# Six homes for the transforms' channel groups, and the resizing products of both spectra later in the text

## The chip, the cores and the metric

The kernel runs on one core of a Trainium2 chip. TensorE (PE) multiplies matrices into PSUM, VectorE (DVE), ScalarE (ACT) and GpSimd (POOL) work on the elements, and SyncE (SP) only issues transfers; DMA transfers are also issued from the queues of ACT and POOL. PE loads its weights by instructions of their own (PEld). All engines run side by side, each through its own instructions in their order, and wait for each other on semaphores.

The metric is the device time of one execution in microseconds (us). Three executions of the kernel before took 9171.22, 9193.05 and 9202.3 us; the median, 9193.05, is the time before. The profile is of a further execution.

## The reference

The input is x, 32 images of 96 channels, 56x56, in float32. Two layers follow each other.

The first layer is a residual block: a 1x1 convolution to 576 channels, batch norm and silu; a depthwise 3x3 convolution, batch norm and silu; a squeeze (mean over the image, two small matrices, sigmoid) that scales the 576 channels; a 1x1 convolution back to 96 channels, batch norm, and x added. The weights go through a fake quantisation to 8 bits first.

The second layer takes the magnitude of an image's spectrum twice. Cut to what matters:

```
mag = abs(rfft2(x));  fe = mag.mean over channels
ca  = sigmoid(W2 relu(W1 pooled(conv(mag))))            # one factor a channel
s   = [x.mean(channels), sqrt((x*x).mean(channels) + 1e-6), resize(fe, 56x56)]
sa  = sigmoid(small convolutions of s)                  # one factor a pixel
y   = x * ca * sa
freq = resize(abs(rfft2(y)).mean over channels, 56x56)
aux = [y, 4 coordinate planes, freq]
offset, gate = 3x3 convolutions of aux;  y_base = 3x3 convolution of y
y_def = deformable 3x3 convolution: y sampled bilinearly at 9 offset taps
z   = (1 - gate) * y_base + gate * y_def
out = relu(batchnorm(z over the whole batch) + x)
```

Since the batch norm takes its statistics over all 32 images, the output is written in a last pass.

## The kernel before

The program has two streams of preparation and one main loop. The main loop goes through bands: an image is cut into 7 bands of 8 rows, 32 images make 224 bands, and each band is joined from offset and gate convolutions (L606), the base convolution (L635), hat tables that turn bilinear sampling into products (L671 to L699), transposes (L714), samples (L728, evacuated to `v` by ACT in L732 and L739) and deformable products (L747).

Beside the bands run two generators, `first(b + 2)` and `second(b + 1)`. `first` is the residual block's expansion and depthwise convolution (`hidden`, L169 to L262), whose result `h2d` goes to DRAM. `second` is `attend`: it loads the rows of `h2d` (`project_loads`, tiles `hq0` and `hq1`, L306), projects them (L324, L330), adds the residual, stores the block's result in DRAM (`x1`, L467/468), and then runs the attention of the second layer. The main loop calls `pump()` at each of the 119 slots of an image; `pump()` steps both generators in proportion to the time: a stream has a number of steps, a slot at which it begins and a slot at which it is due. `second` is due at `slot + length - 8`.

`attend` uses the transform `dft_mag` twice, once on x1 and once on y (with `gate=sa`). A transform has these steps:

- It loads 6 groups of 2 x 8 channels, [112 x 8 x 56], into padded tiles of [112 x 8 x 64] (L362). Three such tiles, `x2_0` to `x2_2`, are filled with zeros once by GpSimd at the start of the program and taken in rotation, so that group g + 3 can only be loaded when group g has been read. Groups 0 to 2 are requested at the transform's start, group g + 3 behind the products of group g.
- For y, GpSimd multiplies each group by sa (`weigh`, L367).
- PE multiplies each group by the first Fourier matrix (L387, four program products a group; the trace shows each fp32 product as two records), into a PSUM bank; ACT copies the result to `s1` (L394). For x1, ACT also squares the group into a PSUM bank (L371) and DVE sums the group and its squares over the channels (L373).
- PE applies the second Fourier matrix in three groups (L411), ACT squares (L414) into a tile of the pool `sq`, DVE adds (L415).
- ACT takes the square root (L418).

`resized_spectrum` follows: DVE (for y) multiplies by the channel factors `cx` (L427) and sums over the channels (L428, `m_fe` or `m_fy`), PE applies the resizing matrix (L431) and ACT copies the result (L433, `fe` or `fy`). `fe` is read much later, in the small convolutions of `s` (L532 onward); in between DVE works out the channel attention (`edge` to `qs`, L486 to L498) and PE multiplies it through (L502, L508, L513), all in columns of one PSUM tile `pc`. `fy` is read by the next product (L573, `pz`), whose copy `fq` (L575) is stored by GpSimd's queue (L578) and loaded as one of the rows of aux (L597) for L606 of the next image.

PSUM has 8 banks: 6 in the rotating pool `mm` (taken by L169, L324, L371, L387, L411, L606, L635, L714, L728, L770), one in `acc` (the small products, L431 among them), one in `pd` (L747). SBUF pools of one buffer: `hq`, `sp`, `sq`, `s1p`; so the next user of such a tile waits for the last reader of the one before.

The order of the instructions on PE, DVE, ACT and POOL is set by a scheduler with a cost model of its own, which may move an instruction past others; SP's instructions stand in the order of the text. A `yield` in a generator sets how the two streams and the bands interleave in that text.

Of the kernel before, what the change touches and what calls it, by code (L numbers as in the profile page):

```python
# [7 lines left out]
FP = mybir.dt.float32  # L8
# [8 lines left out]
C, H, W = 96, 56, 56  # L17
HW = H * W
HID, RED = 576, 24
NCH = 5  # L20
# [13 lines left out]
EW = ER * W  # L34
# [25 lines left out]
CG = 8  # L60
# [240 lines left out]

def project_loads(nc, p, h2d, q, half):

    u0, u1 = ((0, NCH - 1), (NCH - 1, len(UNITS)))[half]
    hq = p["hq"].tile([128, u1 - u0, EW], FP, name=f"hq{half}")
    nc.sync.dma_start(hq, h2d[u0:u1, :, q * EW : (q + 1) * EW].rearrange("u p n -> p u n"))  # L306
    return [(UNITS[u][0], hq[:, u - u0]) for u in range(u0, u1)]
# [31 lines left out]
def dft_mag(nc, p, src, gate=None):  # L339
# [14 lines left out]
    x2s = []  # L354

    def load(g):
        if g < NG:
            x2 = p["x2"][p["n_x2"] % len(p["x2"])]
            p["n_x2"] += 1
            for half in range(2):  # L360
                c0 = half * C // 2 + g * CG
                nc.sync.dma_start(x2[half * H : (half + 1) * H, :, :W], hwc[:, c0 : c0 + CG])  # L362
            x2s.append(x2)
# [58 lines left out]
def resized_spectrum(nc, p, mag, name, scale=None):  # L422


    m2 = p["sp"].tile([2 * WX, V], FP, name=f"m_{name}")
    if scale is not None:
        nc.vector.tensor_tensor(mag, mag, scale.unsqueeze(2).to_broadcast([2 * WX, NP, V]), ALU.mult)  # L427
    nc.vector.tensor_reduce(m2, mag.rearrange("p q u -> p u q"), AX.X, ALU.add)  # L428
    yield
    pf = p["acc"].tile([128, 512], FP, name="acc")  # L430
    nc.tensor.matmul(pf[:V, : 2 * W], m2, p["w"]["RT2"], start=True, stop=True)  # L431
    rs = p["sp"].tile([V, 2, W], FP, name=name)
    nc.scalar.copy(rs.rearrange("p m w -> p (m w)"), pf[:V, : 2 * W])  # L433
    p["resized"] = rs
    yield


def attend(tc, p, b, x, h2d, pooled, x1, given=False):
# [43 lines left out]
    yield from resized_spectrum(nc, p, mag, "fe")  # L482
    fe = p["resized"]
# [28 lines left out]

    nc.tensor.matmul(pc[:C, 1:2], w["cp2"], c1[:MID], start=True, stop=True)  # L513
# [55 lines left out]
    yield from resized_spectrum(nc, p, p["magnitude"], "fy", cx)  # L569
    fy = p["resized"]  # L570
# [352 lines left out]
def padded(nc, p, a, images):  # L923

    cp = p["cp"]
    yps = [cp.tile([CJ, HY, WY], FP, name=f"yp{i}") for i in range(images)]
    for t in yps:
        nc.gpsimd.memset(t, 0.0)
        nc.sync.dma_start(t[C : C + 4, PD : PD + H, PD : PD + W], a["coord"])
        nc.sync.dma_start(t[CA:, PD : PD + H, PD : PD + W], a["place"])  # L930
    p["x2"], p["n_x2"] = [cp.tile([2 * H, CG, WX], FP, name=f"x2_{i}") for i in range(3)], 0
    for t in p["x2"]:
        nc.gpsimd.memset(t, 0.0)
    p["s4"] = [cp.tile([H, 3, WP], FP, name=f"s4_{i}") for i in range(2)]
    for t in p["s4"]:
        nc.gpsimd.memset(t, 0.0)
    return yps
# [8 lines left out]
def layers(tc, a, dp, x1d, zd, stats, far):  # L946
# [8 lines left out]
    with ExitStack() as ctx:  # L955
# [8 lines left out]
                                 ("ca", 2), ("s1p", 1), ("xc", 2), ("sp", 1), ("sq", 1), ("q1", 3), ("q2", 2), ("hid", 2), ("yb", 4),  # L964
# [11 lines left out]
        def second(b):  # L976
            if b >= B:
                return iter(())
            h2d, pooled = held.pop(b)
            return attend(tc, p, b, a["x"][b], h2d, pooled, x1d[b])  # L980
# [34 lines left out]
        def start(b, length):  # L1015
            streams[:] = [[second(b + 1), 0, n_second, slot + 3, slot + length - 8],
                          [first(b + 2), 0, n_first, slot, slot + length]]
# [238 lines left out]
def gather_block(tc, a, dp, x1d, zd, stats):  # L1256
# [4 lines left out]
    with ExitStack() as ctx:  # L1261
# [11 lines left out]
        pools(tc, ctx, p, None, (("ca", 1), ("s1p", 1), ("xc", 2), ("sp", 1), ("sq", 2), ("q1", 2), ("q2", 2),  # L1273
# [235 lines left out]
```

## Time and profile before

| | |
|---|---|
| median of 3 runs | 9193.05 us (9171.22 to 9202.3) |
| profiled execution: device time, span | 9212.26 us, 9210.5 us |
| mean granted clock of TensorE | 0.931 |
| PE busy, instructions | 8288.6 us (90%), 52406 |
| DVE busy | 7178.9 us (78%) |
| ACT busy | 5374.1 us (58%) |
| POOL busy | 2600.3 us (28%) |
| L362, loads of the groups | 768 issues of 98 KB each |
| L387, product of a group | 3072 records, 262 to 562 ns, median 275 |
| L431, resizing product, fe and fy | 64 records each, median 258 and 391 ns |
| L428, sum over the channels | 64 of 2520 to 2585 ns |
| L418, square root, and the table load ahead of it | 1.41 and 1.28 us in the second transform of one image |

The page gives the busy time of each engine, then the span in 40 slices with a digit of the busy share for each. A busy PE is not PE at its peak: matmul records overlap, their ends are modelled, and the clock that the chip grants to TensorE varies; the clock's slices (PEclk) stand in tenths of full speed. A row of the waits reads "engine, line, what it waited for: us in all, times, longest". A wait on an engine that isn't late for anybody costs nothing. A row of the timeline reads "start, duration, engine, line, operation, output <- inputs, count, [idle before <- what ended it]".

### The profile page before, as it was taken

The numbers are of one execution on the slowest core, as the hardware profiler recorded it, in microseconds if no ns is written. First come the engines' busy times: TensorE is split into PE (matmuls) and PEld (weight loads), VectorE is DVE, ScalarE is ACT, GpSimd is POOL, SyncE is SP. The second block draws the span as 40 slices with busy tenths as digits, with TensorE's granted clock in tenths as the row PEclk, the third lists the DMA queues.
The fourth block names the chain that finished last, engine by engine and source line by source line (L and its number), as shares of the span: only waits on it lengthen the run. The fifth ranks groups of instructions, "written<-read, shape, count | busy, mean of one in ns | idle before, by whom it ended". The sixth has DMA issues, their size and how long they took to land. (4 is left out here: it accounts for less than half of the span.)

```text
span 9210.5 us, 138071 instructions
## 1 busy us (share of the span) xinstructions
PE 8288.6 (90%) x52406; PEld 5229.5 (57%) x52406; DVE 7178.9 (78%) x6693; ACT 5374.1 (58%) x10486; POOL 2600.3 (28%) x2611
## 2 busy tenths in 40 slices
PE   5889999999999999999999999999999999999870
PEld 3455556565555656555565655555565556655550
DVE  7587888888788888888888888788888888887333
ACT  2355656666556666665566666566666656666553
POOL 0123233232323323232332333233223323332210
PEclk9889999999999999999999999999999999999985
DMA  2345655555556555555555555555555565555459
GB/s 85 94 136 158 165 167 161 160 154 152 157 164 167 162 158 152 153 158 164 166 162 162 151 152 161 163 165 157 161 147 157 159 166 166 161 164 140 127 181 418
DMA packets 1068764, 1486.54 MB, mean 161 GB/s; under 512 B 590190, under 2 KB 839838, under 8 KB 1055806
## 3 DMA queue, kind: packets, MB, share of 16 engines
q1 hardware_dynamic: 858995, 985.20, 40.1%
q10 hardware_dynamic: 153803, 329.80, 9.8%
q0 software_dynamic: 55296, 162.60, 6.8%
q8 instruction: 421, 6.90, 0.4%
q14 instruction: 249, 2.04, 0.1%
HBM read 1064.29 MB, written 412.65 MB: 160 GB/s over the span
## 5 line engine op out<-in xcount | busy, mean ns | idle before, releaser
L262 DVE SCALAR_TENSOR_TENSOR acch<-hp,w,acch 128x1512 f32<-128x1512 f32 (+1 forms) x2250 | 4397.4, 1954 | 35.7
L606 PE MATMUL mm<-yp,c_jointW 104*128 104x448 f32 x4032 | 1721.4, 580 | 4.8 <-DMA yp<-fqd 2.8
L710 POOL COPY ybl<-yp 96x448 f32<-96x448 f32 x896 | 1133.9, 1292 | 1736.1 <-PE mm L714 1735.9
L747 PE MATMUL pd<-v,c_def 128*96 128x224 f32 (+1 forms) x6272 | 1397.0, 370 | 17.8 <-ACT v L732 16.9
L606 PEld LDWEIGHTS mm<-yp,c_jointW 104*128 104x128 f32 x4032 | 796.9, 201 | 809.7 <-issue 775.0
L747 PEld LDWEIGHTS pd<-v,c_def 128*96 128x96 f32 (+1 forms) x6272 | 1028.3, 170 | 296.5 <-issue 78.5
L728 PE MATMUL mm<-wc,yt 64*96 64x144 f32 x12544 | 1093.4, 301 | 101.2 <-ACT hp L173 45.3
L173 ACT ACTIVATE hp<-mm,sh,inv 128x392 f32<-128x392 f32 (+2 forms) x1216 | 812.8, 673 | 567.3 <-PE mm L169 489.2
L169 PE MATMUL mm<-xt,w 96*128 96x392 f32 (+3 forms) x2688 | 1071.6, 537 | 37.8 <-DMA xt<-in_x 33.3
L728 PEld LDWEIGHTS mm<-wc,yt 64*96 64x96 f32 x12544 | 848.0, 164 | 416.8 <-issue 190.0
L732 ACT COPY v<-mm 96x288 f32<-96x288 f32 (+1 forms) x2688 | 1004.3, 443 | 98.9 <-PE mm L728 60.1
L699 DVE TENSOR_TENSOR wc<-wc,wr 128x1008 f32<-128x1008 f32 x448 | 575.2, 1284 | 570.1 <-DMA wr<-hd 515.7
L324 PE MATMUL mm<-hq,w3s 128*96 128x392 f32 x2048 | 800.8, 538 | 148.2 <-DMA hq<-h2d 145.8
L635 PE MATMUL mm<-yp,c_base0W 96*64 96x224 f32 x8064 | 827.7, 357 | 0.0
L739 ACT COPY v<-v 32x448 f32<-32x448 f32 x1344 | 755.2, 562 | 29.9
L635 PEld LDWEIGHTS mm<-yp,c_base0W 96*64 96x64 f32 x8064 | 553.6, 135 | 276.1 <-issue 71.6
L659 POOL DMA_DIRECT2D od<-at x224 | 185.9, 830 | 1788.0 <-DVE at L655 1247.6
L716 ACT COPY yt<-mm 128x384 f32<-128x384 f32 (+1 forms) x896 | 350.2, 440 | 520.4 <-PE mm L714 519.6
L324 PEld LDWEIGHTS mm<-hq,w3s 128*96 128x96 f32 x2048 | 341.2, 175 | 505.3 <-issue 472.7
L222 ACT ACTIVATE acch<-acch,sh,inv 128x1568 f32<-128x1568 f32 x288 | 488.5, 1696 | 192.4 <-DVE acch L262 182.3
L626 ACT ACTIVATE hid<-mm,c_dg1b 50x448 f32<-50x448 f32 x224 | 140.6, 627 | 744.3 <-PE mm L606 703.2
L467 POOL TENSOR_TENSOR o<-o,xc 96x392 f32<-96x392 f32 x256 | 369.6, 1444 | 677.3 <-ACT o L334 675.9
(194 smaller groups left out, 9065.7 us busy)
## 6 DMA issues: line engine op xcount, KB each, us to landing
h2d<-acch ACTq DMA_DIRECT2D x288, 784.0 KB
wc<-hd SPq DMA_DIRECT2D x896, 252.0 KB
wr<-hd SPq DMA_DIRECT2D x896, 252.0 KB
hq<-h2d SPq DMA_DIRECT2D x128, 980.0 KB
hq<-h2d SPq DMA_DIRECT2D x128, 784.0 KB
x<-x1d SPq DMA_DIRECT2D x768, 98.0 KB
ht<-od SPq DMA_DIRECT2D x224, 252.0 KB
hd<-ht ACTq DMA_DIRECT2D x224, 252.0 KB
```

The costliest lines, as they stand in the source:

```text
L169: nc.tensor.matmul(pt[p0 : p0 + w1.shape[1], : rows * W], w1, xts[hf][:, r0 * W : (r0 + rows) * W], start=True, stop=True)
L173: nc.scalar.activation(h1[lo:hi, row0 : row0 + rows, 1 : 1 + W], pt[lo:hi, : rows * W].rearrange("p (h w) -> p h w", h=rows), AF.Silu, bia ...
L262: nc.vector.scalar_tensor_tensor(acc[:, lo:hi], win, wk, acc[:, lo:hi], ALU.mult, ALU.add)
L324: nc.tensor.matmul(pts[half][:C, :EW], w3s[:, ch], hq, start=(i == 0), stop=False)
L606: nc.tensor.matmul(view, weights[:, k], yp[:channels, r0 : r0 + RB, dx + PD - 1 : dx + PD - 1 + W], start=(k == 0), stop=(k == NTAP - 1))
L635: nc.tensor.matmul(pb[i * BC : (i + 1) * BC, : BW // 2].rearrange("p (h w) -> p h w", h=RB // 2), w["base"][:, k], yp[:C, r0 + i * RB // 2 ...
L699: p["tc"].keep_in_program_order(nc.vector.tensor_tensor(wc, wc, wr, ALU.mult))
L710: nc.gpsimd.tensor_copy(yb[:, :, s], blocks)
L728: nc.tensor.matmul(pt[k][:C, (t - lo) * KP : (t - lo + 1) * KP], yt[ps, t], s[ps, t * KP : (t + 1) * KP], start=True, stop=True)
L732: nc.scalar.copy(v[:C, :, lo:hi, k].rearrange("c k t p -> c t k p"), pt[k][:C, : (hi - lo) * KP].rearrange("c (t k p) -> c t k p", t=hi - ...
L739: nc.scalar.copy(v[C:, 1 + 2 * i : 3 + 2 * i], v[i * QC : (i + 1) * QC, KA:])
L747: nc.tensor.matmul(out.rearrange("c q (t x) -> c t q x", x=TS), p["w"]["def"][ks, k], v[ks, k].rearrange("c t s (r x) -> c t (s r) x", r=T ...
```

## The change

The three tiles `x2_0` to `x2_2` go. Instead the six groups of a transform live in the two tiles of the projection's rows: groups 0 to 2 in `hq0`, groups 3 to 5 in `hq1`, each taken anew at the transform's start (a function `project_rows` gives the tile for both uses). As these tiles hold other data in between, the padding columns 56 to 63 of all six groups are zeroed by DVE at each transform's start: two memsets of [112 x 24 x 8] a transform.

The pool `sq` gets two buffers in place of one.

`resized_spectrum` is split. `summed_spectrum` keeps the scaling and the sum over the channels at their old place; the resizing product and its copy come later in the text. For fe they now stand after L508 (new numbers: the product is L440), directly ahead of the product of the channel attention's last matrix (L513, new L523), and the product writes columns 128 and up of the PSUM tile `pc`, not a tile of its own. For fy they stand one step later than before. `second` has one step more and is due at `slot + length - 6`.

A block at the end of the program that doesn't run for these inputs gets a pool `hq`, as `dft_mag` asks for it.

```diff
--- before.py
+++ after.py
@@ -299,10 +299,15 @@
     yield
 
 
+def project_rows(p, half):
+
+    return p["hq"].tile([128, (NCH - 1, len(UNITS) - NCH + 1)[half], EW], FP, name=f"hq{half}")
+
+
 def project_loads(nc, p, h2d, q, half):
 
     u0, u1 = ((0, NCH - 1), (NCH - 1, len(UNITS)))[half]
-    hq = p["hq"].tile([128, u1 - u0, EW], FP, name=f"hq{half}")
+    hq = project_rows(p, half)
     nc.sync.dma_start(hq, h2d[u0:u1, :, q * EW : (q + 1) * EW].rearrange("u p n -> p u n"))
     return [(UNITS[u][0], hq[:, u - u0]) for u in range(u0, u1)]
 
@@ -352,15 +357,16 @@
     if gate is None:
         parts = p["sq"].tile([2 * WX, 2, NPB * V], FP, name="sq")[: 2 * H, :, : NG * W].rearrange("p k (g w) -> p k g w", g=NG)
     x2s = []
+    for i in range(2):
+        rows = project_rows(p, i).rearrange("p u n -> p (u n)")[: 2 * H, : NG // 2 * CG * WX].rearrange("h (c w) -> h c w", w=WX)
+        nc.vector.memset(rows[:, :, W:], 0.0)
+        x2s.extend(rows[:, g * CG : (g + 1) * CG] for g in range(NG // 2))
 
     def load(g):
         if g < NG:
-            x2 = p["x2"][p["n_x2"] % len(p["x2"])]
-            p["n_x2"] += 1
             for half in range(2):
                 c0 = half * C // 2 + g * CG
-                nc.sync.dma_start(x2[half * H : (half + 1) * H, :, :W], hwc[:, c0 : c0 + CG])
-            x2s.append(x2)
+                nc.sync.dma_start(x2s[g][half * H : (half + 1) * H, :, :W], hwc[:, c0 : c0 + CG])
 
     def weigh(g):
         if gate is not None and g < NG:
@@ -419,20 +425,22 @@
     p["magnitude"] = mag
 
 
-def resized_spectrum(nc, p, mag, name, scale=None):
+def summed_spectrum(nc, p, mag, name, scale=None):
 
 
     m2 = p["sp"].tile([2 * WX, V], FP, name=f"m_{name}")
     if scale is not None:
         nc.vector.tensor_tensor(mag, mag, scale.unsqueeze(2).to_broadcast([2 * WX, NP, V]), ALU.mult)
     nc.vector.tensor_reduce(m2, mag.rearrange("p q u -> p u q"), AX.X, ALU.add)
-    yield
-    pf = p["acc"].tile([128, 512], FP, name="acc")
+    return m2
+
+
+def resized_spectrum(nc, p, m2, name, pf):
+
     nc.tensor.matmul(pf[:V, : 2 * W], m2, p["w"]["RT2"], start=True, stop=True)
     rs = p["sp"].tile([V, 2, W], FP, name=name)
     nc.scalar.copy(rs.rearrange("p m w -> p (m w)"), pf[:V, : 2 * W])
-    p["resized"] = rs
-    yield
+    return rs
 
 
 def attend(tc, p, b, x, h2d, pooled, x1, given=False):
@@ -479,8 +487,9 @@
     nc.scalar.activation(s3[:, 1], pm[:H, W : 2 * W], AF.Sqrt, bias=w["eps6"][:H], scale=1.0 / C)
     nc.scalar.mul(s3[:, 0], pm[:H, :W], 1.0 / C)
     yield
-    yield from resized_spectrum(nc, p, mag, "fe")
-    fe = p["resized"]
+    m_fe = summed_spectrum(nc, p, mag, "fe")
+    yield
+    yield
     mas = p["sp"].tile([2 * WX, 2, NP], FP, name="mas")
     edge = p["sp"].tile([2 * WX, NP, NE], FP, name="edge")
     nc.vector.tensor_copy(edge[:, :, :4], mag[:, :, :4])
@@ -510,6 +519,7 @@
     nc.scalar.activation(c1, pc[: 2 * MID, 0:1], AF.Relu, bias=w["cp1b"])
     yield
 
+    fe = resized_spectrum(nc, p, m_fe, "fe", pc[:, 128:])
     nc.tensor.matmul(pc[:C, 1:2], w["cp2"], c1[:MID], start=True, stop=True)
     c2 = p["sp"].tile([2 * MID, 2 * WX], FP, name="c2")
     nc.vector.tensor_scalar(c2, w["twoT"], c1, None, ALU.mult)
@@ -566,8 +576,11 @@
 
     yield from dft_mag(nc, p, x1, sa)
     yield
-    yield from resized_spectrum(nc, p, p["magnitude"], "fy", cx)
-    fy = p["resized"]
+    m_fy = summed_spectrum(nc, p, p["magnitude"], "fy", cx)
+    yield
+    yield
+    fy = resized_spectrum(nc, p, m_fy, "fy", p["acc"].tile([128, 512], FP, name="acc"))
+    yield
     pz = p["acc"].tile([128, 512], FP, name="acc")
     for m in range(2):
         nc.tensor.matmul(pz[:H, H : H + W], w["rows2"][:, m], fy[:, m], start=(m == 0), stop=(m == 1))
@@ -928,9 +941,6 @@
         nc.gpsimd.memset(t, 0.0)
         nc.sync.dma_start(t[C : C + 4, PD : PD + H, PD : PD + W], a["coord"])
         nc.sync.dma_start(t[CA:, PD : PD + H, PD : PD + W], a["place"])
-    p["x2"], p["n_x2"] = [cp.tile([2 * H, CG, WX], FP, name=f"x2_{i}") for i in range(3)], 0
-    for t in p["x2"]:
-        nc.gpsimd.memset(t, 0.0)
     p["s4"] = [cp.tile([H, 3, WP], FP, name=f"s4_{i}") for i in range(2)]
     for t in p["s4"]:
         nc.gpsimd.memset(t, 0.0)
@@ -961,7 +971,7 @@
         top = p["cp"].tile([NOFF, NBD + 1], FP, name="top")
         nc.gpsimd.memset(top, 0.0)
         pools(tc, ctx, p, None, (("xt", 2), ("acch", 2), ("pl", 2), ("w3s", 1), ("hq", 1), ("o", 2), 
-                                 ("ca", 2), ("s1p", 1), ("xc", 2), ("sp", 1), ("sq", 1), ("q1", 3), ("q2", 2), ("hid", 2), ("yb", 4),
+                                 ("ca", 2), ("s1p", 1), ("xc", 2), ("sp", 1), ("sq", 2), ("q1", 3), ("q2", 2), ("hid", 2), ("yb", 4),
                                  ("off", 1), ("st", 2), ("ht", 1), ("wc", READY + AHEAD + 1), ("wr", AHEAD + 1), ("yt", 2), ("ybl", 1),
                                  ("vp", 2)))
 
@@ -1013,7 +1023,7 @@
         turn = NBD - 2
 
         def start(b, length):
-            streams[:] = [[second(b + 1), 0, n_second, slot + 3, slot + length - 8],
+            streams[:] = [[second(b + 1), 0, n_second, slot + 3, slot + length - 6],
                           [first(b + 2), 0, n_first, slot, slot + length]]
 
         def pump():
@@ -1270,7 +1280,7 @@
             tz = table.rearrange("(p n) f -> p (n f)", p=116)
             for i in range(4):
                 nc.sync.dma_start(tz[:, i * zt.shape[1] : (i + 1) * zt.shape[1]], zt)
-        pools(tc, ctx, p, None, (("ca", 1), ("s1p", 1), ("xc", 2), ("sp", 1), ("sq", 2), ("q1", 2), ("q2", 2),
+        pools(tc, ctx, p, None, (("ca", 1), ("s1p", 1), ("xc", 2), ("sp", 1), ("sq", 2), ("hq", 1), ("q1", 2), ("q2", 2),
                                  ("hid", 2), ("off", 1), ("ix", 2), ("vp", 1), ("gp", 4), ("smp", 2)))
         with tc.For_i(0, B, 1) as b:
             st = p["sp"].tile([C, NBD, 6], FP, name="st")
```

## The prediction

> **What bounds the kernel now.** I read the page's busy shares and slices first, then the waits of TensorE (PE), of VectorE (DVE), of ScalarE (ACT) and of SyncE's queue (SP), then the timeline of one image.
>
> ```profile
> PE 8288.6 (90%) x52406; PEld 5229.5 (57%) x52406; DVE 7178.9 (78%) x6693; ACT 5374.1 (58%) x10486; POOL 2600.3 (28%) x2611
> PE   5889999999999999999999999999999999999870
> PEclk9889999999999999999999999999999999999985
> ```
> PE is busy 9 tenths or more in nearly every slice, at a clock that reads 9, not 10. So time comes back only from PE's idle stretches, from the slow stretches behind them, or from DVE where PE follows it. Which idle stretches does the change touch?
>
> ```profile
> PE mm L324 <- DMA hq<-h2d: 145.8, 30, 7.0
> PE acc L431 <- DVE m_fe L428: 64.0, 31, 2.7
> PE mm L387 <- DVE sq L373: 54.9, 19, 4.2
> PE acc L431 <- DVE m_fy L428: 51.7, 32, 11.3
> PE mm L387 <- DMA x<-x1d: 42.7, 13, 11.0
> PE mm L387 <- POOL x L367: 18.1, 29, 3.4
> ACT sq L414 <- DVE s L415: 216.7, 50, 7.2
> SPq L362 <- PE mm L387: 924.8, 124, 50.7
> ```
> Columns: microseconds in all, times, longest. The largest, L324 for its rows, is not touched. L431, the resizing product, is both times PE's next instruction while DVE still sums the spectrum: 64.0 and 51.7 us over 31 or 32 images. SP's 924.8 us at the transforms' loads is a queue's wait; only its readers' idle time counts.
>
> The first transform's end, one image (start, duration, in brackets the idle time before):
> ```profile
> 1119.77 2.56 DVE L428 TENSOR_REDUCE m_fe<-s 128x29 f32<-128x1392 f32 x1
> 1122.48 0.55 PE L431 MATMUL acc<-c_RT,m_fe 128*29 128x112 f32 x2 [2.21 <-DVE m_fe L428]
> 1122.95 10.12 PE L606 MATMUL mm<-yp,c_jointW 104*128 104x448 f32 x18
> 1133.77 0.39 DVE L655 COPY at<-mm 18x224 f32<-18x224 f32 x1 [1.88 <-ACT hid L626]
> 1137.32 0.29 DVE L498 TENSOR_TENSOR qs<-qs 128x144 f32<-128x144 f32 x1
> 1138.91 0.43 PE L502 MATMUL acc<-c_two,qs 128*48 128x2 f32 x6
> ```
> PE idles 2.21 us; then its 18 joint products take 10.12 us. At 1196.17 the same 18 take 7.03. The window of these 10 us (busy PE, weights, DVE, ACT, POOL, then the granted clock) says why:
> ```profile
> 1120.00:1130.00 10.00, 7.79 (x14) 3.53 (x14) 10.00 (x9) 7.19 (x13) 0.27 (x1) 0.66 0.20 81
> ```
> The clock is 0.66; in the next 10 us it is 1.00. So a stall of 2 us drags a half-speed stretch behind it that costs about 3 us more. The trace's stretches at 0.5 are mostly 6.8 us long, so one that PE fills costs 6.8/2 = 3.4 us. DVE pays too: it waits 1.88 us at L655 for what PE delivers late, and L498 (qs), which L502 reads, moves with it.
>
> The squares' bank in the same image:
> ```profile
> 1078.75 2.44 PE L747 MATMUL pd<-v,c_def 128*96 128x224 f32 x12
> 1080.30 1.21 DVE L699 TENSOR_TENSOR wc<-wc,wr 128x1008 f32<-128x1008 f32 x1 [5.91 <-DMA wr<-hd]
> 1082.37 1.15 DVE L373 TENSOR_REDUCE sq<-mm 112x56 f32<-112x448 f32 x2
> 1083.04 1.15 PE L387 MATMUL mm<-c_FU,x 112*128 112x116 f32 x8 [1.86 <-DVE sq L373]
> ```
> Group 3 of the first transform needs a PSUM bank that DVE's L373 must empty, and DVE sits 5.91 us in L699 on a hat table's DMA (wr).
>
> The second transform's end:
> ```profile
> 1216.25 2.56 DVE L428 TENSOR_REDUCE m_fy<-s 128x29 f32<-128x1392 f32 x1
> 1217.10 0.73 PE L728 MATMUL mm<-wc,yt 64*96 64x144 f32 x6 [1.51 <-ACT hp L173]
> 1218.87 0.58 PE L431 MATMUL acc<-c_RT,m_fy 128*29 128x112 f32 x2 [1.04 <-DVE m_fy L428]
> ```
> PE's 1.51 us before L728 are ACT's (square root and table loads); only the 1.04 us at L431 are the spectrum's.
>
> **The change part by part**, per image of about 268 us, 31 of them in the steady part. The order of instructions is read from the two programs.
>
> *Six homes (hq0, hq1) for the groups.* The same 768 loads issue in the same order on SP; those of groups 3 to 5 no longer wait for L387, L371, L373 or (second transform) L367. What they let forward on SP, the hat tables (L692, L693), stands ahead of them and is held by hd's DMA (974.2 us at L692), so L699 stays as it is. Group 3's stall stays too: in most images its last releaser is the bank (L373). In 10 images between 700 and 8000 us the load was (22.7 us at L387), which now comes early; the bank comes free nearly then, so 0 (at best -0.7). The first groups' loads still wait for x1's store (755.0 us on SP). Project's rows share the buffers: the loads of both kinds gain PE waits, but those readers are a stage away, so nothing; if not, L306's rows get late and L324's 145.8 us grow. What can go is the 18.1 us at L387 for GpSimd (POOL), which weighed late because the load came late: -0.3 an image (0 to -0.6). In the first image PE is half idle (slices 5 and 8), and loads that come early may save 6 us once (0 to 15; the longest waits at L387 for a load are 11.0).
>
> *Memsets.* 4 an image more on DVE, [112x24x8], 3 large ones less on POOL at the start. The nearest rows are DVE's copy of 128x192 at 0.25 us and a memset of 64x58 at 0.11: 0.4 to 1.0 in all. The first stands before an L260 that waits for ACT (270.4 us over 88), the second and fourth among short z operations. I take +0.1 (0 to +1.0 if DVE's idle time doesn't cover them).
>
> *Two buffers for the squares.* ACT's L414 loses its wait for L415, 216.7 us in all. ACT idles 42% of the span, and PE named L414 for 3.0 us at L411 in all: 0 (-0.5 to +0.2, as ACT's squares now run ahead of the expansions' L173).
>
> *Deformable products behind the group.* With the buffers free the scheduler puts FU groups 3 and 4 ahead of 3 or 4 of the 7 L747 program products that stood before group 3. A record of L747 takes 2.44/12 = 0.20 us and a program product is two: 3 x 0.4 = 1.2. They filled PE while the bank was held; now PE idles through that and runs them later, on the path to L411 (DVE's L415 waits 114.9 us for L414, so PE leads there): +1.2 (0, if the third inverse group has slack, to +1.6).
>
> *The first resize later (L440 in the new file).* PE meets L606 instead of the sum and doesn't stall 2.2 us. Work between L431 and L502 at full clock is 16.4 us (1122.5 to 1138.9) less about 3.1 of slow L606 less the product's own 0.6, and PE now starts it 2.2 earlier: it reaches L502 10.7 us after the sum's end (1122.33), while it needs qs: 15.3 us here, less the 1.88 at L655: 13.4. So PE waits at L502 instead, 2.7 us. What is late next is therefore PE again, two steps on, with a slow stretch behind it. L502 starts 13.5 after the sum instead of 15.3 in the mean of the images: -1.8, of which a slow stretch in half of the images gives back 3.4/2 = 1.7. What surely stays is DVE's wait at L655, 1.0 in the mean. The product and its copy (0.22 us) now lie in the bank `pc`, between L508 and L513; L513 waits for the copy with one L169 and one L728 between: +0.2. Together I take -0.8 (from -3.9, if stall and slow stretch both go, to +1.0).
>
> [...]
>
> *The second resize later.* The next six L728 (6 records, 0.73 us; so 12 records, 1.5) run before L431 and cover the 1.04; in the mean 51.7/32 = 1.6, the first image's 11.3 left out 1.3. Then L573 must wait for the copy L433, which on ACT now stands behind five or so more evacuations (0.42 us each), with 3 or 4 L747 as its cover. The stored row's way (fq, L578, L597) gets some 2 us longer; L606 waited only 2.8 us for it in all. The stall by ACT stays, and with it most of the slow stretch. I take -0.9 (-2.7 if a stretch goes too in half of the images, to +0.8 if L573 waits). `second` being due two slots later belongs to this.
>
> Sum: -0.3 + 0.1 + 0 + 1.2 - 0.8 - 0.9 = -0.7 an image; x 31 = -22, with the start's 6: -28 us. Against the profiled execution's own time, 9212.3, that is 9184; the median of the runs is 19 us lower, so 9165.
>
> **The rivals.**
> *A: stalls and slow stretches both go.* For it: the slow stretches seen start behind gaps like these. Against: qs bounds L502, and ACT's gap stays. Price, with the lows of both resizes, POOL's -0.3, 0.3 for memsets and L513, and L747 absorbed: -3.9 - 2.7 - 0.3 + 0.3 = -6.6 x 31 = -205: 8990.
> *B: the stall only changes place.* L502 and L573 give back all that L431 loses, and the L747 find slack: 0, 9193.
> *C: slower, at group 3.* The displaced L747 lengthen the bank's stall from 1.9 to 3.1 us, and a slow stretch more follows in half the images: 1.6 + 1.7 = 3.3 in the place of 1.2, the sum -0.7 becomes +1.4: x 31 less the start's 6 = +37, 9230. It decides once L411's third group comes more than 2 us later behind group 3 than now. For it: DVE's wait for L414, 114.9 us. Against: DVE is as loaded behind the transform (8.5 to 10 of 10 us), and PE may catch up unseen.
>
> **How the numbers follow.** What a measurement of this kernel can tell from no change is 0.3%, 27.6 us. Mine (9165, own range 9125 to 9195) has 0.45, A 0.12, B 0.18, C 0.25. Mine lies on the bound: 0.28 faster, 0.17 same. A is faster; B 0.02 faster, 0.14 same, 0.02 slower; C 0.02 same, 0.23 slower. Together 0.42, 0.33 and 0.25. The lows of all terms sum to -8.4 an image, the highs to +4.6; half way from -0.7 to each is -4.6 and +1.95, with the start 9046 and 9247. C's heavier half belongs inside, A's far half needn't: 9070 to 9260.
>
> **What would show it.** Right: L431 gone from PE's waits (both rows under 10 us); L502 with some 60 to 80 us for L498; L655's 170.8 less by 30; group 3's row for L373 grown by 35; L324 unchanged near 146; L699's 515.7 unchanged; POOL's 18.1 near nothing; the mean clock between 0.925 and 0.935. It would be wrong if the clock goes above 0.94 (A), if L502 shows no wait (then DVE got faster than I read), if L324 or L606 show new DMA waits (the shared buffers or the later row), or if L411 or L513 appear with more than 20 us.

## The result and the profile after

The changed kernel takes 9224.38 us in the median of 20 runs, the kernel before 9198.62 in 20: a ratio of 1.0025, 95% interval 1.0016 to 1.0033. The forecast was 9165; the change is a small loss, not a small gain. The profiled execution after has a span of 9211.6 us at a mean clock of 0.934 (before: 9210.5, 0.931); it is one of the changed kernel's quicker ones (its runs go from 9194.8 to 9245.05), so totals are compared by medians and places by the traces.

TensorE's waits after (us in all, times, longest):
```profile
PE mm L329 <- DMA hq<-h2d: 144.9, 31, 6.6
PE mm L393 <- DVE sq L379: 94.1, 22, 5.6
PE acc L511 <- DVE qs L507: 76.6, 30, 2.7
PE mm L727 <- POOL ybl L723: 59.1, 29, 2.8
PE mm L619 <- DMA yp<-fqd: 45.3, 23, 3.2
PE acc L586 <- ACT fy L442: 34.2, 28, 1.7
PE acc L440 <- DVE m_fy L434: 14.3, 3, 6.4
PE mm L741 <- ACT hp L173: 8.4, 13, 1.0
```
New lines for old ones: L329 is L324, L393 is L387, L379 is L373, L511 is L502, L727 is L714, L619 is L606, L586 is L573, L440 is L431, L741 is L728. The wait for m_fe is gone and 76.6 us for qs stand in its place; m_fy's 51.7 is 14.3, and the 45.3 that L728 waited for hp are 8.4. But the bank at group 3 went from 54.9 to 94.1, and three waits are new or much larger: 59.1 for GpSimd's copies, 45.3 for the stored row (2.8 before), 34.2 for fy's copy.

One sum orders all that follows. I cut each trace into images at the squeeze's first product (L285), took 26 images of the steady part, and added for each the time in which neither PE nor its weight loads were busy and the time at half clock:

| an image, us | period | PE idle | at half clock | idle + half/2 | period less that |
|---|---|---|---|---|---|
| before | 268.69 | 14.64 | 26.91 | 28.10 | 240.59 |
| changed | 269.69 | 17.28 | 25.86 | 30.21 | 239.48 |

The last column is 238.9 to 241.5 in all 18 kernels of this study. So PE's work in an image is about 240 us at full clock, and the rest is idle time plus half of the slow time. The change added 2.6 us of idle time and took 1.0 of slow time away. The gain lies in the first two images: the third one begins 21 us earlier (664 us after the start, 685 before), and the steady images lose it again.

### The profile page after: what moved, and what is told of

Same layout as the page of the kernel before. It is cut to its first block, busy times and chain, and to the rows that moved or that the text cites. A ratio compares the mean times of both kernels' runs of the same rounds, so it can differ in the third digit from the quotient of the medians.

```text
span 9211.6 us, 138241 instructions
## 1 busy us (share of the span) xinstructions
PE 8244.4 (90%) x52406; PEld 5240.2 (57%) x52406; DVE 7126.2 (77%) x6821; ACT 5372.9 (58%) x10486; POOL 2746.8 (30%) x2608
## 5 line engine op out<-in xcount | busy, mean ns | idle before, releaser
L262 DVE SCALAR_TENSOR_TENSOR acch<-hp,w,acch 128x1512 f32<-128x1512 f32 (+1 forms) x2250 | 4336.9, 1928 | 33.0
L619 PE MATMUL mm<-yp,c_jointW 104*128 104x448 f32 x4032 | 1675.7, 567 | 45.6 <-DMA yp<-fqd 45.3
L760 PE MATMUL pd<-v,c_def 128*96 128x224 f32 (+1 forms) x6272 | 1430.8, 374 | 22.5 <-ACT v L745 14.9
L619 PEld LDWEIGHTS mm<-yp,c_jointW 104*128 104x128 f32 x4032 | 777.0, 196 | 839.7 <-issue 781.6
L760 PEld LDWEIGHTS pd<-v,c_def 128*96 128x96 f32 (+1 forms) x6272 | 1029.4, 171 | 324.0 <-issue 103.0
L712 DVE TENSOR_TENSOR wc<-wc,wr 128x1008 f32<-128x1008 f32 x448 | 579.1, 1293 | 651.1 <-DMA wr<-hd 509.9
L741 PE MATMUL mm<-wc,yt 64*96 64x144 f32 x12544 | 1057.7, 297 | 27.3 <-ACT hp L173 8.4
L741 PEld LDWEIGHTS mm<-wc,yt 64*96 64x96 f32 x12544 | 835.0, 162 | 321.8 <-issue 164.6
L329 PE MATMUL mm<-hq,w3s 128*96 128x392 f32 x2048 | 802.7, 539 | 146.3 <-DMA hq<-h2d 144.9
L329 PEld LDWEIGHTS mm<-hq,w3s 128*96 128x96 f32 x2048 | 341.9, 176 | 504.2 <-issue 471.5
L393 PE MATMUL mm<-c_FU,hq 112*128 112x116 f32 x3072 | 456.2, 298 | 144.7 <-DVE sq L379 94.1
```

The costliest lines, as they stand in the source:

```text
L262: nc.vector.scalar_tensor_tensor(acc[:, lo:hi], win, wk, acc[:, lo:hi], ALU.mult, ALU.add)
L329: nc.tensor.matmul(pts[half][:C, :EW], w3s[:, ch], hq, start=(i == 0), stop=False)
L619: nc.tensor.matmul(view, weights[:, k], yp[:channels, r0 : r0 + RB, dx + PD - 1 : dx + PD - 1 + W], start=(k == 0), stop=(k == NTAP - 1))
L712: p["tc"].keep_in_program_order(nc.vector.tensor_tensor(wc, wc, wr, ALU.mult))
L741: nc.tensor.matmul(pt[k][:C, (t - lo) * KP : (t - lo + 1) * KP], yt[ps, t], s[ps, t * KP : (t + 1) * KP], start=True, stop=True)
L760: nc.tensor.matmul(out.rearrange("c q (t x) -> c t q x", x=TS), p["w"]["def"][ks, k], v[ks, k].rearrange("c t s (r x) -> c t (s r) x", r=T ...
```

## The experiments

All ratios are to the kernel before, which was run beside them on the same chip; five rounds each.

**The parts alone.** Four kernels each take a part of the change. Homes alone: the tiles and memsets of the change, `("sq", 1)`, both products where they were.

> The six homes alone; one buffer for the squares, both resizing products at their old places. Theory H (the homes cost what the resizing products win): the two stalls that are new or larger with the change come with this part: group 3 of the first transform waits 3.5 to 4 us an image for DVE's squares (2.4 before), and the transposes wait about 2 us for GpSimd's ybl copies, which now stand behind six weighings in a row; with their slow stretches the time is 40 to 120 us above the kernel before. Rival R (the moved resizing products cost, the homes are neutral): within 20 us of the kernel before, and no row of transposes waiting for ybl over 20 us.

First product alone (the three rotating tiles stay):
```diff
+    m_fe = summed_spectrum(nc, p, mag, "fe")
+    yield
+    yield
...
+    fe = resized_spectrum(nc, p, m_fe, "fe", pc[:, 128:])
     nc.tensor.matmul(pc[:C, 1:2], w["cp2"], c1[:MID], start=True, stop=True)
```


> Only the first resizing product moved behind L508 into the bank of the channel attention. Both theories: the 64 us at the product for m_fe go, 70 to 80 us at the product of the channel attention's first step (for qs) come. H: within 25 us of the kernel before, as the stall and its slow stretch only change place. R: 20 to 60 us slower.

Second product alone, with its due slot:
```diff
+    m_fy = summed_spectrum(nc, p, p["magnitude"], "fy", cx)
+    yield
+    yield
+    fy = resized_spectrum(nc, p, m_fy, "fy", p["acc"].tile([128, 512], FP, name="acc"))
+    yield
...
-            streams[:] = [[second(b + 1), 0, n_second, slot + 3, slot + length - 8],
+            streams[:] = [[second(b + 1), 0, n_second, slot + 3, slot + length - 6],
```


> Only the second resizing product moved one step later, and the stream due two slots later. H: PE's 2.5 us an image at the end of the second transform and the slow stretch of 8.5 us behind it mostly go (-3 to -4 us an image with the new waits for fy and for the stored row fq counted), so 60 to 120 us faster than the kernel before. R: the joint products waiting for the fq row (45 us in all) and the product of fy waiting for its copy (34 us) take all of it, so 0 to 60 us slower.

Both products:

> Both resizing products moved, the stream due two slots later, the groups in their three rotating tiles and one buffer for the squares. H: 50 to 120 us faster than the kernel before, the sum of the two parts alone. R: 20 to 90 us slower.

| | ratio, 95% | PE idle | at half clock | idle + half/2 |
|---|---|---|---|---|
| homes | 0.9977 (0.9966 to 0.9988) | 16.46 | 22.97 | 27.94 |
| first product | 1.0052 (1.0038 to 1.0066) | 15.09 | 27.96 | 29.07 |
| second product | 1.0145 (1.0129 to 1.016) | 19.88 | 26.12 | 32.94 |
| both products | 1.0224 (1.0209 to 1.0239) | 20.36 | 30.72 | 35.72 |

Theory H fell. I had seen the two waits that the homes bring, and they are there (67.7 us for the bank, 56.4 for GpSimd's copies), and still the homes alone are a gain, while both products lose. What the second product alone does is in its waits of PE:
```profile
PE mm L392 <- POOL x L372: 142.1, 45, 5.0
PE mm L618 <- DMA yp<-fqd: 50.8, 23, 4.0
PE acc L585 <- ACT fy L441: 35.6, 28, 1.7
```
L392 is the group's product, L372 GpSimd's weighing: 18.1 us before, 142.1 now. R foresaw the two lower rows, not this one, and though it had the first product's loss (20 to 60 us, measured 46), it had no row of transposes waiting for GpSimd's copies and a loss of at most 90 us for both products, which is 207. The four ratios don't add up to the changed kernel either, so the parts depend on each other.

**One part left out.** The changed kernel without its first move, without its second move (and due slot), without both, and with one buffer for the squares.

> The changed kernel with the first resizing product back at its old place (homes, two buffers for the squares, second product later). Theory I (the parts depend on each other: the second product's move is dear only while the second transform's groups come late and GpSimd weighs late, and the homes take that wait away; what is left of the change's loss is the first product's move): the 140 us that the second move costs alone do not appear, no row of group products waiting for GpSimd's weighing over 15 us, and the time is 30 to 55 us below the changed kernel (ratio to before 0.997 to 0.9995). Rival J (the second move costs its stalls at the joint products and at the product of fy, about 80 us in all, whatever the homes do; the second buffer for the squares pays for them): within 15 us of the changed kernel, ratio 1.001 to 1.004.

> The changed kernel with the second resizing product and the stream's due slot as before (homes, two buffers, first product later). I: the first move's 45 us on top of the homes' gain of 21: ratio 1.001 to 1.004, within 15 us of the changed kernel. J: 40 to 80 us below the changed kernel, ratio 0.994 to 0.998.

> Homes and the two buffers for the squares, both resizing products as before. I: as the homes alone, which took 0.9977 of the kernel before: 0.996 to 0.999. J: the second buffer brings 40 us or more: below 0.994.

> The changed kernel with one buffer for the squares. I: within 20 us of the changed kernel, ratio 1.001 to 1.005. J: 40 us or more above it, ratio over 1.006, with ScalarE's wait at the squares for VectorE's sum back at 200 us or more.

| | ratio, 95% | PE idle | at half clock | idle + half/2 |
|---|---|---|---|---|
| without the first move | 0.9911 (0.9898 to 0.9924) | 15.97 | 20.74 | 26.34 |
| without the second move | 0.995 (0.9938 to 0.9962) | 16.32 | 23.24 | 27.94 |
| homes and two buffers only | 0.9893 (0.9879 to 0.9907) | 15.83 | 20.09 | 25.87 |
| one buffer for the squares | 1.0075 (1.0062 to 1.0088) | 18.79 | 27.44 | 32.51 |

Both theories miss sizes. Homes and two buffers are a gain of 1.07%, 97 us; the second buffer, which I had put at nothing, is most of it (0.9977 to 0.9893), as J said. ScalarE's wait at the squares for VectorE's sum, with homes and one buffer and then with homes and two:
```profile
ACT sq L420 <- DVE s L421: 148.8, 63, 5.6
ACT sq L420 <- DVE s L421: 2.7, 2, 1.5
```
In the changed kernel with one buffer it is 187.8 (J had 200 or more). That this wait is what the second buffer pays with is argued, not shown: no single wait of PE falls by the 77 us. The moved products take the gain away and more: the first costs 0.57% on top of homes and buffers (0.9893 to 0.995) and 1.14% when the second is moved too (0.9911 to 1.0025); the second costs 0.18% without the first (0.9893 to 0.9911, intervals that overlap) and 0.75% with it. That the second move's 140 us don't appear with the homes is as theory I had it. Two buffers without the homes were not run, so what the second buffer is worth by itself stays open.

**Why the first product's move costs.** In the changed kernel's timeline (start, duration, idle time before):
```profile
1098.08 2.58 DVE L434 TENSOR_REDUCE m_fe<-s 128x29 f32<-128x1392 f32 x1
1098.59 7.02 PE L619 MATMUL mm<-yp,c_jointW 104*128 104x448 f32 x18
1113.80 0.29 DVE L507 TENSOR_TENSOR qs<-qs 128x144 f32<-128x144 f32 x1
1114.14 0.43 PE L511 MATMUL acc<-c_two,qs 128*48 128x2 f32 x6 [2.63 <-DVE qs L507]
1117.21 3.30 PE L760 MATMUL pd<-v,c_def 128*96 128x224 f32 x8
1126.52 0.15 DVE L277 TENSOR_SCALAR ca<-ca 96x1 f32<-96x1 f32 x1 [3.52 <-ACT ca L276]
```
and the window behind the stall (its clock is the third number from the end):
```profile
1115.00:1122.00 7.00, 7.00 (x39) 5.33 (x39) 6.84 (x8) 1.06 (x3) 0.27 (x1) 0.54 0.30 106
```
The 18 joint products now take 7.02 us, not 10.12. PE then stands 2.63 us before qs, and the slow stretch lies on what follows: eight records of L760 take 3.30 us (8 x 0.20 before). They are the work between two links of the channel attention's chain, so its end comes late too, and VectorE waits 3.52 us for `ca`. Over the steady images the stall at m_fe was 2.06 us and a slow stretch followed in 23 of 27 cases, 4.42 us in the mean; with homes and two buffers it is 1.96 us, with a stretch in 12 of 28, 2.19 us. The stall at qs is 2.60 us, with a stretch in 27 of 27, 6.95 us (these means count an image without a stretch as 0). With homes, two buffers and the first product moved, one edit away from homes and two buffers, the stall is 2.59 us, with a stretch in 27 of 27, 6.32 us. Between these two kernels, idle time plus half the slow time grows by 2.5 us in the 40 us that begin 160 us into the image and hold both places, and by 2.1 in the whole image: the loss lies at this stall.

If qs is the cause, an earlier qs should help. In this kernel (homes, two buffers, first product moved) the sum goes behind qs on VectorE, over the half of qs that has been read, and qs' reader one step later:
```diff
-    m_fe = summed_spectrum(nc, p, mag, "fe")
...
     nc.vector.tensor_tensor(qs[:, 0], qs[:, 0], qs[:, 1], ALU.add)
     yield
+    m_fe = qs[:, 1, 0, :V]
+    nc.vector.tensor_reduce(m_fe, mag.rearrange("p q u -> p u q"), AX.X, ALU.add)
+    yield
     pc = p["acc"].tile([128, 512], FP, name="acc")
```


> Homes and two buffers for the squares, second resizing product as before, first product behind L508 as in the change; but the sum m_fe comes behind qs on VectorE (it is written over the half of qs that the last addition has read, so that it can't be pulled ahead), and the step that reads qs stands one step later. Theory Q (the moved first product costs because PE, no longer held at m_fe, runs into qs: 2.6 us and a slow stretch in nearly every image): with qs some 2.5 us earlier, the wait for it falls under 30 us in all (76.6 in the changed kernel), the slow stretch behind it goes in most images, and the time is at or below that of homes and two buffers with the product at its old place: ratio 0.980 to 0.990. Rival S (it costs because the product and its copy stand in the bank and in the chain of the channel attention, ahead of L513): ratio 0.993 to 0.998, as with homes, two buffers and the first product moved (0.995).

Measured: 1.0035 (1.0021 to 1.0048). The wait for qs is gone (2.5 us, once), as Q said, and the time is worse than either theory had it. Its waits of PE show where the stall went:
```profile
PE acc L544 <- DVE cx L534: 58.0, 29, 2.7
```
L544 (L532 before) stands further down the same chain; there PE idles 2.00 us an image in the mean and the slow stretches behind it are the longest seen, 10.24 us in the mean. The images alternate: a stall of some 2.55 us is followed by some 10 us at half clock each time, one of 1.48 us either by none or by 20 to 24 us. Idle time is the second lowest of all kernels until then (14.72), time at half clock the highest (32.56). So PE seems to be ahead of VectorE by about 2 us all along this chain (2.06 us at m_fe, 2.60 at qs, 2.00 here), and taking away one wait handed it to the next link. But this version also has one step more in the stream, and the traces show that much of its loss is that step's: L742's wait for hp at the second transform's end, 7.3 us in the kernel it was made from (0.995), is back at 38.4. Of the 3.1 us by which idle time plus half the slow time grew against that kernel (27.94 to 31.00), 1.7 lie in the 60 us around this chain and 2.1 between the second transform's end and the next image's first 20 us; the rest of the image gains 0.7. Rival S isn't excluded by the time, but leaves little in the trace: in the changed kernel no matmul of L523 (L513 before) waits for fe's copy, its weight loads do for 9.7 us in all.

**Where the homes' gain and loss lie.** From homes and two buffers (0.9893), six homes in one of the two transforms and three in the other:
```diff
-    for i in range(2):
+    deep = 2 if gate is None else 1
+    for i in range(deep):
...
+    x2s *= 2 // deep
```
(for six homes in the second transform only, the condition is `gate is not None`).

> As homes and two buffers (0.9893), but six homes only in the first transform; the second takes three, in rotation. Theory: the gain of the homes lies at the second transform's end, where PE had 2.5 us of waits and a slow stretch of 8.5 us an image before; with three homes that stretch comes back, GpSimd's ybl copies are no longer waited for (53 us go), and the ratio is 0.994 to 1.000. Rival (the gain lies in the first transform or in the squares' buffers): 0.987 to 0.991.

> As homes and two buffers (0.9893), but six homes only in the second transform; the first takes three, in rotation, and the deformable products stay ahead of group 3. Theory: the wait for the squares' bank at group 3 falls from 3.7 to 2.4 us an image, all else stays: 0.984 to 0.989. Rival (the bank's wait ends on VectorE's time anyway, and the products are done behind it unseen): 0.988 to 0.992.

Only in the first: 0.9927 (0.9911 to 0.9944), between the two forecasts. Only in the second: 0.986 (0.9846 to 0.9875), as forecast and the best kernel of the study, 9084.86 us in the median beside 9208.94, with 15.25 us idle and 19.17 at half clock an image. It beats both the kernel before and the changed one. With three homes in the second transform the stall at its end is back, as the waits of that kernel (homes in the first only) show:
```profile
PE mm L742 <- ACT hp L173: 44.4, 30, 1.5
PE acc L442 <- DVE m_fy L436: 37.5, 28, 9.3
PE mm L742 <- ACT yb L654: 22.7, 28, 0.9
```
(44.4 and 22.7; before 45.3 and 21.8), with some 8 us at half clock in its 20 us, where six homes have 1. So the gain of the homes is the second transform's end, reached sooner. With three homes in the first transform the deformable products stay ahead of group 3, and the stall there is 2.58 us in the steady images, not 3.98; a stretch follows in 16 of 28, not in 27 of 28. The waits of the kernel with homes in the second only:
```profile
PE mm L395 <- DVE sq L381: 58.9, 23, 4.2
PE mm L728 <- POOL ybl L724: 50.6, 29, 2.5
PE mm L620 <- DMA yp<-fqd: 37.0, 21, 4.8
```
Its first row is 97.2 with six homes in both. The second row is the price of the early loads that I had missed. In the changed kernel's timeline GpSimd, no longer held by the buffers, weighs all six groups before the copies that the transposes need:
```profile
1145.72 9.28 POOL L373 TENSOR_TENSOR hq<-hq,sa 112x448 f32<-112x448 f32 x4
1155.50 2.14 POOL L373 TENSOR_TENSOR hq<-hq,sa 112x448 f32<-112x448 f32 x1
1158.98 1.24 POOL L373 TENSOR_TENSOR hq<-hq,sa 112x448 f32<-112x448 f32 x1
1160.17 6.32 POOL L723 COPY ybl<-yp 96x448 f32<-96x448 f32 x2
1166.54 0.80 PE L727 MATMUL mm<-c_ident,ybl 96*128 96x96 f32 x7 [1.65 <-POOL ybl L723]
```
Can that be had back? Four homes in the second transform hold the last two weighings:
```diff
-    x2s *= 2 // deep
+    homes = 4 if gate is not None else 3
+    x2s = [x2s[g % homes] for g in range(NG)]
```


> As six homes in the second transform only (0.986), but four in place of six: groups 4 and 5 wait for groups 0 and 1, and GpSimd does four weighings, then ybl copies, then the last two. Theory P (the transposes' wait for ybl, 50.6 us, and the slow stretch behind it come from the row of weighings): that wait falls under 20 us, ratio 0.979 to 0.985. Rival (the early weighings are what brings the transform's end forward, so that the stall at its end returns): ratio 0.989 to 0.994.

Measured: 0.9949 (0.9931 to 0.9968). The wait for the copies is gone from the leading waits of PE, and the stall at the transform's end is back in its place:
```profile
PE mm L743 <- ACT hp L173: 45.3, 31, 1.5
PE mm L743 <- ACT yb L655: 45.3, 38, 1.8
```
P had the wait right and the time wrong; the rival had the mechanism. The early groups are the gain (this run holds back loads and weighings together, so it doesn't tell the two apart), and the wait for the copies is its smaller price.

**Why the second move costs 140 us alone.** It is two edits, a step and a due slot. Each alone on the kernel before:
```diff
-            streams[:] = [[second(b + 1), 0, n_second, slot + 3, slot + length - 8],
+            streams[:] = [[second(b + 1), 0, n_second, slot + 3, slot + length - 6],
```


> Only the due slot moved from length - 8 to length - 6; both products at their old places. D: ratio 1.006 to 1.017, with group products waiting 80 us or more for GpSimd. W: 0.997 to 1.003.

> Only the second resizing product moved one step later, the stream due at its old slot (length - 8). Theory D (the due slot shifts the second transform against the bands, so that GpSimd's weighings of groups 3 to 5 fall behind the ybl copies): most of the 140 us go, ratio 0.997 to 1.004, and the row of the group products waiting for GpSimd is under 50 us. Rival W (the product's own waits, for fy's copy and the stored row): ratio 1.011 to 1.017, waits as in fy_only.

The due slot alone: 1.0508 (1.049 to 1.0526), 9676.72 us beside 9216.9, by far the largest effect here. The step with the old due slot: 1.0222 (1.02 to 1.0244). Together they were 1.0145. By the program's text a later due time stretches the stream over more slots, and a further step presses it together, so that the two partly cancel; that is argued from the text. With the due slot alone there is no one culprit, by its waits:
```profile
PE mm L387 <- POOL x L367: 108.2, 46, 5.1
PE mm L728 <- DVE sq L373: 81.0, 32, 3.1
PE mm L606 <- DMA yp<-fqd: 78.3, 24, 5.7
PE pd L747 <- ACT v L739: 67.3, 14, 6.7
```
Idle time goes from 14.64 to 26.53 us an image, half clock from 26.91 to 38.73. D was right that the due slot weighs, though its cost is three times the 1.7% that D allowed, and about GpSimd's row. It was wrong in that the step alone is dear as well, with GpSimd's row larger still, where D had it under 50:
```profile
PE mm L392 <- POOL x L372: 196.4, 51, 6.3
```

Do the homes and buffers make the alignment harmless? The same edit on homes and two buffers, and the due slot moved the other way (`length - 10`) on the best kernel:

> Six homes and two buffers for the squares, both products at their old places, the stream due at length - 6. Theory A (step and due slot cancel in the alignment; the homes do not make it harmless): ratio 1.005 to 1.04, with transposes or group products waiting 80 us or more for GpSimd. Rival B (the homes make the transform insensitive to two slots): 0.988 to 0.996.

> Six homes in the second transform alone and two buffers for the squares (0.986), the stream due at length - 10. A: the alignment moves off its best place, 0.990 to 1.03. B: 0.983 to 0.989; the joint products' wait for the fq row, 37 us, falls as the row is stored earlier.

They don't: 1.0203 (1.0186 to 1.022) where 0.9893 stood, and 1.0076 (1.0048 to 1.0104) where 0.986 stood. With the later slot on homes and two buffers the joint products wait 101.7 us for the stored row and L440 87.6 for m_fy, in that kernel's waits:
```profile
PE mm L618 <- DMA yp<-fqd: 101.7, 30, 5.5
PE acc L440 <- DVE m_fy L434: 87.6, 32, 3.4
PE mm L740 <- DVE sq L379: 75.9, 30, 2.9
```
A had the times, not the row: transposes and group products wait 22.9 and 4.4 us for GpSimd in the first of the two. With homes and buffers the slot alone thus costs 3.1 points, and slot and step together 0.18 (0.9893 to 0.9911); the step alone was not run with them. Why two slots cost so much was shown only as far as these rows. That every meeting of the transforms with the bands shifts is how I read them.

## Why the prediction was wrong

The forecast gain became a loss at the two moved products: -0.8 and -0.9 an image forecast, together -1.7; on top of homes and buffers they measured 0.9893 to 1.0025, which is 121 us or +3.9 an image. The step that failed is the slow stretch behind L502, taken in half of the images where it came in all: the first move costs 0.57 to 1.14% on that ground. With it fell the forecast for the second move, whose due slot had no price: not a gain but a loss of 0.18 to 0.75%. Homes and buffers were wrong the other way: +1.0 forecast with the deformable products, -3.1 measured (97 us). That the two errors nearly cancel, so that the time came within 60 us of the forecast, is luck. Term by term:

- *Two buffers for the squares: 0 forecast.* This is the largest wrong term among those that came out better than forecast. I read that ACT's wait at L414 named few PE waits, and left it at that. On top of the homes it is worth 0.84% (0.9977 to 0.9893), about 77 us or 2.5 an image: 0.6 less idle time and 2.9 less half clock. The bound of -0.5 was too narrow.
- *The homes: -0.2 forecast, +1.0 with the deformable products; -0.7 measured with them, for another reason.* POOL's wait at L387 did go (18.1 to 6.1), but the waits for a load there, which were to end earlier, mostly stayed (42.7 us to 34.6), and 59.1 us at the transposes came in POOL's place; I followed the loads on SP and not what GpSimd, once free to weigh, is ahead of. The gain that outweighs this, the second transform's end, I had put down to the second product's move; and I had written that "the stall by ACT stays": L728's waits for hp and yb, 45.3 and 21.8 us, are 8.4 and 1.7 in the changed kernel, and 2.3 for hp with the homes alone. The start's 6 us were 21.
- *Deformable products behind group 3: +1.2 forecast.* Right in place and near in size (the stall ahead of group 3 goes from 2.63 to 4.09 us in the steady images). Undoing it in homes and two buffers brought 0.33% (0.9893 to 0.986), 30 us, or 1.0 an image.
- *The first resize: -0.8 forecast; alone +0.52%, some +1.5 an image.* The new stall was forecast at 2.7 us and is 2.60, and L502 starts 13.5 us behind the sum, as forecast (15.5 before). The term that failed is "a slow stretch in half of the images": it follows in all, and 6.95 us long where the old one had 4.42. That is (6.95 - 4.42)/2 + (2.60 - 2.06) = 1.8 us lost, where I had a gain. The gain was also summed wrongly: L655's 1.0 is already in the 13.5 at which L502 starts, and was taken off a second time, and the pieces as written make -0.9, not -0.8.
- *The second resize: -0.9 forecast; alone +1.45%, with homes and buffers +0.18%.* The stall for m_fy goes as forecast (51.7 to 14.3), and the waits I had at 0 to 0.8 came: 34.2 us for fy's copy and 45.3 for the stored row, where I had counted 2.8 in all. Of the stored row's, 37.3 are there with homes and two buffers alone, so the move is not their only cause. That `second` is due two slots later had no price at all, and that edit alone is 5%. Why it costs so much stays open; shown are the waits that grow.
- *Rivals.* A's stretches did go at the second transform's end, but new ones came. B's mechanism, stalls that change place, is nearest to what happened to the first product. C's stall came near its price; its slow stretch too (4.93 to 7.59 us behind group 3), but the loss was bought back by the buffers, which no rival had. That C's 9230 is the number nearest to 9224 is luck: the loss lies at the moved products, not at group 3.

Of the signs to look for, L431's row for m_fe is gone, and the one for m_fy is 14.3, not under 10. L502's 60 to 80 us (76.6), group 3's growth by 35 (39), L324 (144.9), L699 (509.9) and the clock (0.934) came as written. L655's wait fell by 11, not 30. Of the warnings, L606's new wait for a DMA came.

## What to carry to other kernels

Here a stall that was taken away at one instruction came back at the next one that needed the slower engine (64.0 us for m_fe became 76.6 for qs, and with qs earlier 58.0 for cx); follow the chain to its end and ask how long the stall will be there: with homes and two buffers, one of 1.96 us was followed by half clock in 12 of 28 images, and with the first product moved as well, one of 2.59 in 27 of 27. Length is not all, as the stalls at L544 show, where one of 1.48 us was followed either by none or by 20 to 24 us. Price an edit of a due time or of a step count by a run: as I read it, it moves every meeting of two interleaved streams, and two slots of 119 cost more than any other edit here (1.0508). When a buffer frees an engine that was held back, look at what that engine now does first, and who waits for what it does later: here the transposes, 59.1 us for GpSimd's copies.

## What the runs showed of the hardware

In these traces half clock followed an idle gap of PE the more often the longer the gap was: behind 1% of the gaps of 0.5 to 1.25 us, behind 99.8% of those over 3.0. Over the 18 traces, for single idle gaps of PE (no other of over 0.5 us within 9 us, clock full before, 700 to 8000 us), the share that was followed by a stretch at 0.5 was:

| gap, us | gaps | followed by half clock |
|---|---|---|
| 0.5 to 1.25 | 222 | 1% |
| 1.25 to 1.75 | 326 | 40% |
| 1.75 to 2.0 | 309 | 55% |
| 2.0 to 2.5 | 241 | 73% |
| 2.5 to 3.0 | 250 | 95% |
| over 3.0 | 866 | 99.8% |

The half clock began 1.7 to 4.7 us after the gap's start (10th to 90th of a hundred). Nearly all the stretches lasted 3.41, 6.83 or 10.24 us (859, 1110 and 430 of 2539). Gaps of 1.25 to 1.75 us were enough in two cases of five here. The table is a count, not a test: these gaps differ in place and in the work behind them as well as in length. The prediction read the clock behind one stall, of 2.21 us, and took half of the images for a stall of 2.7; of the gaps of 2.5 to 3.0 us here 95% were followed.
